# Longer stores for long rows, eight pairs shared by ScalarE and GpSimd, and short rows made on VectorE, in a store-bound kernel

## Chip, cores, metric

One core of one Trainium2 chip. The metric is the device time of one execution in microseconds (us), the median of several runs.

## The reference

For every pair (row r, column c < r) of 39 fields it forms the outer product of two 16-vectors, normalizes over the batch, and multiplies by a 16x16 weight.

```python
cross  = xj[:, rows, :, None] * xi[:, cols, None, :]         # (1024, 741, 16, 16)
mean   = jnp.mean(cross, axis=(0, 2, 3), keepdims=True)
var    = jnp.mean(jnp.square(cross - mean), axis=(0, 2, 3), keepdims=True)
normed = (cross - mean) * jax.lax.rsqrt(var + BN_EPS)
normed = normed * gamma[None, :, None, None] + beta[None, :, None, None]
out    = normed[:, :, None, :, :] * W[None, None, :, :, :]   # 777 MB in float32
```

With s and t for scale and shift of a pair, the work is `(xj * (xi * s) + t) * W`. The loads move 6 MB and the stores 777 MB, so the kernel is above all a stream of stores.

## The kernel before

The statistics take the first 40 us. Then the kernel goes through tiles (row r, two samples of each of 128 partitions). A long row r and the short row 38 - r share a *slot*: 38 pairs, one half of a double buffer in SBUF. Every pair of one sample is 1 KB per partition.

- `scale_xi` (GpSimd): xs = xi * s.
- `products`: xs * xj, 16 small operations per sample, 11 or 12 on ScalarE, the others on GpSimd.
- `finish`: (y + t) * W, one VectorE operation per pair (0.66 us); a few pairs on GpSimd instead, as one add each and one joint weighting.
- `store`: pieces of the tile as they become ready, all on SyncE's queue.

```python
def products(n):
    xs = xs_of.pop(n)
    split = E - (POOL_I_LONG if tiles[n][0] > TWO else POOL_I)
    for t in range(T):
        for i in range(E):
            product(n, nc.scalar if i < split else nc.gpsimd, t, i, xs[:, t])

def store(n, c0, c1):
    # [cut]
    step = 1 if r > ONE and c1 == r else T      # the last piece leaves sample by sample
    for t in range(0, T, step):
        nc.sync.dma_start(out_v[...], view(n)[:, t : t + step, c0:c1, :])

def bounds(n):
    # [cut: the first eight tiles]
    pieces = 1 + (r > ONE) + (r > TWO)          # ONE, TWO = 24, 31

# the main loop
    if n + 2 < len(tiles):
        scale_xi(n + 2)
    finish(n)
    # [cut]
    if n + 1 < len(tiles):
        products(n + 1)
```

In the timelines below each engine executes its own instructions in the order in which this loop emits them: GpSimd idles 8.16 us before an add while its next products stand behind it, and they start earlier when they are emitted earlier (e5).

## Time and profile before

| | before |
|---|---|
| time, median of 6 runs | 1891.22 us |
| VectorE, ScalarE, GpSimd busy | 92%, 86%, 83% |
| store queue, share of its 16 engines | 98.3% |
| DMA packets | 70288 |

An engine's busy share is an average; the row to look at first is the DMA's. A queue that is busy for 98% of the span sets the time, and an engine's idle time beside it costs nothing, until the engine delivers a store so late that the queue runs dry. The prediction below shows the lines for this.

### The profile page before, as it was taken

Reading aid. Unit: us, or ns where it says so; the run is one execution under the profiler, and the core shown is the slowest. Engines: PE = TensorE matmul, PEld = TensorE weight load, DVE = VectorE, ACT = ScalarE, POOL = GpSimd, SP = SyncE. Lnnn points to the kernel's source line nnn. Section 1 sums busy time; section 2 is a strip of 40 time slices with the busy share of each in tenths; the row PEclk is TensorE's granted clock in tenths of the full one; section 3 lists DMA queues with packets and bytes.
Section 4 is the critical chain, followed back from the end, with each engine's and each line's share of the span. In section 5 each row is a group of like instructions: output and inputs, shape, how many; then the busy total and the mean of one; then the engine's idle time right before and its main releaser. Section 6 shows DMA issues by size and latency. Waiting matters only on the chain. (4 is left out here: it accounts for less than half of the span.)

```text
span 1889.3 us, 10288 instructions
## 1 busy us (share of the span) xinstructions
PE 24.5 (1%) x128; PEld 23.1 (1%) x128; DVE 1730.7 (92%) x2612; ACT 1621.3 (86%) x3625; POOL 1574.5 (83%) x1985
## 2 busy tenths in 40 slices
PE   3100000000000000000000000000000000000000
PEld 3100000000000000000000000000000000000000
DVE  7999999998989898989898989899999999999996
ACT  8999989898989898989898989888888888888762
POOL 9798878788888888888888888888888888888972
DMA  4999999999999999999999999999999999999999
GB/s 164 390 418 429 425 427 429 430 424 429 424 425 426 424 424 426 422 425 425 424 425 423 426 423 426 422 422 422 421 421 422 418 415 419 416 419 419 415 419 390
DMA packets 70288, 783.67 MB, mean 415 GB/s; under 512 B 5057, under 2 KB 6209, under 8 KB 15937
## 3 DMA queue, kind: packets, MB, share of 16 engines
q1 hardware_dynamic: 69632, 780.46, 98.3%
q10 hardware_dynamic: 576, 2.56, 0.3%
q14 instruction: 79, 0.64, 0.1%
q8 instruction: 1, 0.02, 0.0%
HBM read 6.00 MB, written 776.99 MB: 414 GB/s over the span
## 5 line engine op out<-in xcount | busy, mean ns | idle before, releaser
L238 DVE SCALAR_TENSOR_TENSOR y_sb<-y_sb,st_sb,w_dve 128x512 f32<-128x512 f32 x2542 | 1678.5, 740 | 131.5 <-issue 128.3
L139 ACT ACTIVATE y_sb<-xs,xj_sb 128x256 f32<-128x256 f32 (+32 forms) x3544 | 1576.4, 539 | 223.5 <-DMA out_dram<-y_sb 171.8
L141 POOL TENSOR_SCALAR y_sb<-xs,xj_sb 128x560 f32<-128x560 f32 (+35 forms) x1256 | 643.2, 536 | 35.1 <-DMA out_dram<-y_sb 32.6
L230 POOL TENSOR_TENSOR y_sb<-y_sb,w_sb 128x1024 f32<-128x1024 f32 (+4 forms) x138 | 442.0, 3203 | 11.5
L159 POOL TENSOR_TENSOR xs<-xi_sb,st_sb 128x576 f32<-128x576 f32 (+37 forms) x150 | 187.8, 1252 | 225.3 <-ACT y_sb L139 217.8
L226 POOL TENSOR_SCALAR y_sb<-y_sb,st_sb 128x512 f32<-128x512 f32 x384 | 259.4, 692 | 12.9 <-ACT y_sb L139 12.9
L204 DVE TENSOR_TENSOR y_sb<-y_sb,w_dve 128x2560 f32<-128x2560 f32 (+5 forms) x8 | 21.0, 2682 | 2.3 <-ACT y_sb L194 2.3
L139 ACT ACTIVATE y_sb<-xi_sb,xj_sb 128x304 f32<-128x304 f32 x40 | 18.7, 534 | 0.1
L414 PE MATMUL ps<-y_sb 39*128 39x38 f32 (+37 forms) x76 | 16.5, 397 | 5.6 <-DVE y_sb L402 5.6
L414 PEld LDWEIGHTS ps<-y_sb 39*128 39x128 f32 x76 | 16.3, 329 | 5.8 <-issue 5.8
L194 ACT ACTIVATE y_sb<-y_sb,st_sb 128x512 f32<-128x512 f32 x20 | 14.2, 797 | 0.0
L196 POOL TENSOR_SCALAR y_sb<-y_sb,st_sb 128x512 f32<-128x512 f32 x18 | 13.5, 771 | 0.3 <-issue 0.3
L141 POOL TENSOR_SCALAR y_sb<-xi_sb,xj_sb 128x304 f32<-128x304 f32 x24 | 11.9, 518 | 0.0
L299 DVE TENSOR_REDUCE y_sb<-y_sb 128x78 f32<-128x1248 f32 x8 | 11.1, 1442 | 0.0
L277 DVE TENSOR_REDUCE y_sb<-xj_sb 128x78 f32<-128x1248 f32 (+1 forms) x5 | 5.9, 1189 | 5.6 <-DMA xj_sb<-in_r_xj_dram 5.6
L293 ACT ACTIVATE y_sb<-y_sb 128x1248 f32<-128x1248 f32 x8 | 9.9, 1243 | 1.3 <-POOL y_sb L283 1.1
L283 POOL TENSOR_TENSOR y_sb<-xj_sb,y_sb 128x1248 f32<-128x1248 f32 x4 | 9.3, 2314 | 1.9 <-ACT y_sb L327 1.9
L283 POOL TENSOR_TENSOR y_sb<-xi_sb,y_sb 128x1248 f32<-128x1248 f32 x4 | 9.3, 2318 | 0.0
L316 PE MATMUL ps<-y_sb 128*39 128x79 f32 x48 | 7.2, 339 | 16.5 <-DVE y_sb L299 16.5
L316 PEld LDWEIGHTS ps<-y_sb 128*39 128x39 f32 x48 | 6.1, 183 | 17.4 <-DVE y_sb L299 9.6
L277 DVE TENSOR_REDUCE y_sb<-xi_sb 128x78 f32<-128x1248 f32 (+1 forms) x5 | 5.9, 1186 | 0.0
L259 POOL TENSOR_SCALAR_AFFINE_SELECT y_sb<-y_sb 39x4992 f32<-39x4992 f32 x1 | 4.6, 4623 | 0.0
(45 smaller groups left out, 16.9 us busy)
## 6 DMA issues: line engine op xcount, KB each, us to landing
out_dram<-y_sb SPq DMA_DIRECT2D x32, 3072.0 KB, 13.7
out_dram<-y_sb SPq DMA_DIRECT2D x28, 2816.0 KB, 15.7
out_dram<-y_sb SPq DMA_DIRECT2D x32, 1664.0 KB, 14.2
out_dram<-y_sb SPq DMA_DIRECT2D x16, 3328.0 KB, 17.2
out_dram<-y_sb SPq DMA_DIRECT2D x30, 1536.0 KB, 15.2
out_dram<-y_sb SPq DMA_DIRECT2D x12, 3840.0 KB, 17.6
out_dram<-y_sb SPq DMA_DIRECT2D x12, 3584.0 KB, 18.1
out_dram<-y_sb SPq DMA_DIRECT2D x22, 1792.0 KB, 17.4
```

The costliest lines, as they stand in the source:

```text
L139: nc.scalar.activation(y, src, AF.Copy, scale=scale)
L141: engine.tensor_scalar(y, src, scale, 1.0, ALU.mult, ALU.mult)
L159: nc.gpsimd.tensor_tensor(xs, xi_sb[:, t0 : t0 + T, 0:r, :], s_sb[:, :, n0 : n0 + r, :].to_broadcast([P, T, r, E]), ALU.mult,)
L194: nc.scalar.activation(y[:, :, c, :], y[:, :, c, :], AF.Identity, bias=t_c, scale=s_c)
L196: nc.gpsimd.tensor_scalar(y[:, :, c, :], y[:, :, c, :], s_c, t_c, ALU.mult, ALU.add)
L204: nc.vector.tensor_tensor(y[:, :, c0:c1, :], y[:, :, c0:c1, :], w_dve.unsqueeze(1).to_broadcast([P, T, c1 - c0, EE]), ALU.mult,)
L226: nc.gpsimd.tensor_scalar(y[:, :, c, :], y[:, :, c, :], t_sb[:, n0 + c : n0 + c + 1], 1.0, ALU.add, ALU.mult)
L230: nc.gpsimd.tensor_tensor(y[:, :, split:r, :], y[:, :, split:r, :], w_sb.unsqueeze(1).to_broadcast([P, T, r - split, EE]), ALU.mult,)
L238: stt(y[:, :, c, :], y[:, :, c, :], t_sb[:, n0 + c : n0 + c + 1], w_dve.to_broadcast([P, T, EE]), ALU.add, ALU.mult,)
L283: nc.gpsimd.tensor_tensor(devs[n % 7], sources[x][:, t0 : t0 + T], shift[:, x : x + 1, :].unsqueeze(3).to_broadcast([P, T, F, E]), ALU.sub ...
L316: nc.tensor.matmul(acc[0:F, 0 : 2 * F + 1], lhs, fb[:, t], start=t == 0, stop=t == NT - 1)
L414: nc.tensor.matmul(ps[:, :, first[r] - n0 : first[r] - n0 + r], pick[:, r, :], stq[:, :, 0:r], start=True, stop=True,)
```

## The change

Its intent is fewer and longer packets at the end of the run, where rows are long, with the work redistributed so that halves are ready in time. A packet here is what one partition stores of one sample in one piece: 12 pairs are 12 KB. (1) Rows over 31 leave in halves instead of thirds. (2) In rows over 33, ScalarE adds t to eight pairs of the first half, in two fours, and GpSimd weighs them. (3) VectorE scales and multiplies rows 1 to 4 itself, from copies of s and xj in PSUM, with an own buffer. In rows 32 and 33 ScalarE also takes 12 of 16 products again, instead of 11. Cut to its core:

```diff
-ONE, TWO = 24, 31
+ONE, LONG = 24, 33
-POOL_SHARE = 0.13
+POOL_SHARE, POOL_PAIRS_LONG = 0.13, 8
+SHORT = 4
 ...
     def products(n):
+        if r <= SHORT:
+            xs = scaled_short.tile(...)
+            nc.vector.tensor_tensor(xs, xi_sb[...], s_short[...], ALU.mult)
+            for t in range(T):
+                nc.vector.tensor_tensor(view(n)[:, t]..., xs[:, t]..., xj_short[...], ALU.mult)
+            return
 ...
-        split = E - (POOL_I_LONG if tiles[n][0] > TWO else POOL_I)
+        split = E - (POOL_I_LONG if tiles[n][0] > LONG else POOL_I)
 ...
-        pieces = 1 + (r > ONE) + (r > TWO)
+        pieces = 1 + (r > ONE)
 ...
     def finish(n):
-        split = r - int(r * POOL_SHARE + 0.5)
-        for c in range(split, r):
-            nc.gpsimd.tensor_scalar(...)                  # add t
-        if split < r:
-            nc.gpsimd.tensor_tensor(y[:, :, split:r, :], ...)   # weigh
+        long = r > LONG
+        p1 = r // 2 if long else r
+        p0 = p1 - (POOL_PAIRS_LONG if long else int(r * POOL_SHARE + 0.5))
+        step = POOL_PAIRS_LONG // 2 if long else r
+        for c0 in range(p0, p1, step):
+            c1 = min(c0 + step, p1)
+            for c in range(c0, c1):
+                if long:
+                    nc.scalar.activation(y[:, :, c, :], ..., AF.Identity, bias=t_c)
+                else:
+                    nc.gpsimd.tensor_scalar(...)          # add t
+            nc.gpsimd.tensor_tensor(y[:, :, c0:c1, :], ...)     # weigh
         ...
         def apply(group):
-            nc.vector.tensor_mul(st_sb[:, 0, n0:n1], ps[:, 0], st_sb[:, 0, n0:n1])
+            nc.vector.tensor_mul(ps[:, 0], ps[:, 0], st_sb[:, 0, n0:n1])
+            nc.vector.tensor_copy(st_sb[:, 0, n0:n1], ps[:, 0])
 ...
         affine(0)
+        nc.scalar.copy(xj_short, xj_sb[:, :, 1 : SHORT + 1, :])
```

More of the change, by code (lines that the diff above doesn't have):

```diff
@@ L75, in tile_pair_outer_batchnorm @@
     cpool = ctx.enter_context(tc.tile_pool(name="cpool", bufs=1))
+    scaled_short = ctx.enter_context(tc.tile_pool(name="scaled_short", bufs=1))
     scaled = ctx.enter_context(tc.tile_pool(name="scaled", bufs=2))
@@ L124, in tile_pair_outer_batchnorm @@
     ps_s, ps_c, ps_g = banks[0], banks[1], banks[2:5]
+    s_short = ps_g[0]
+    xj_short = ps_c.rearrange("p (t r i) -> p t r i", t=NT, i=E)
     ps_st = banks[5:7] + ps_g
@@ L167, in products @@
     def products(n):
+        r, t0, _ = tiles[n]
+        if r <= SHORT:
+            xs = scaled_short.tile([P, T, r, E], F32, tag="xs_short", name=f"xs_{r}_{t0}")
+            nc.vector.tensor_tensor(
+                xs,
+                xi_sb[:, t0 : t0 + T, 0:r, :],
+                s_short[:, first[r] : first[r] + r]
+                .unsqueeze(1)
+                .unsqueeze(3)
+                .to_broadcast([P, T, r, E]),
+                ALU.mult,
+            )
+            for t in range(T):
+                nc.vector.tensor_tensor(
+                    view(n)[:, t].rearrange("p n (i j) -> p n i j", j=E),
+                    xs[:, t].unsqueeze(2).to_broadcast([P, r, E, E]),
+                    xj_short[:, t0 + t, r - 1 : r, :].unsqueeze(3).to_broadcast([P, r, E, E]),
+                    ALU.mult,
+                )
+            return
         xs = xs_of.pop(n)
-        split = E - (POOL_I_LONG if tiles[n][0] > TWO else POOL_I)
+        split = E - (POOL_I_LONG if tiles[n][0] > LONG else POOL_I)
         for t in range(T):
@@ L223, in finish @@
         y = view(n)
-        split = r - int(r * POOL_SHARE + 0.5)
-        for c in range(split, r):
-            nc.gpsimd.tensor_scalar(
-                y[:, :, c, :], y[:, :, c, :], t_sb[:, n0 + c : n0 + c + 1], 1.0, ALU.add, ALU.mult
-            )
-        if split < r:
+        long = r > LONG
[5 more added lines that the diff above has]
+            for c in range(c0, c1):
+                t_c = t_sb[:, n0 + c : n0 + c + 1]
+                if long:
+                    nc.scalar.activation(y[:, :, c, :], y[:, :, c, :], AF.Identity, bias=t_c)
+                else:
+                    nc.gpsimd.tensor_scalar(
+                        y[:, :, c, :], y[:, :, c, :], t_c, 1.0, ALU.add, ALU.mult
+                    )
             nc.gpsimd.tensor_tensor(
-                y[:, :, split:r, :],
-                y[:, :, split:r, :],
-                w_sb.unsqueeze(1).to_broadcast([P, T, r - split, EE]),
+                y[:, :, c0:c1, :],
+                y[:, :, c0:c1, :],
+                w_sb.unsqueeze(1).to_broadcast([P, T, c1 - c0, EE]),
                 ALU.mult,
@@ L236, in finish @@
         for c0, c1 in zip(bounds(n), bounds(n)[1:]):
-            for c in range(c0, min(c1, split)):
+            for c in [*range(c0, min(c1, p0)), *range(max(c0, p1), c1)]:
                 stt(
```

## The prediction

> **What bounds the kernel now.** I read the page's first parts, then the busy time by stretches, the waits, the timeline of one slot and the groups by form. First the busy shares and the DMA rows of the page:
>
> ```profile
> PE 24.5 (1%) x128; PEld 23.1 (1%) x128; DVE 1730.7 (92%) x2612; ACT 1621.3 (86%) x3625; POOL 1574.5 (83%) x1985
> ...
> DMA  4999999999999999999999999999999999999999
> GB/s 164 390 418 429 425 427 429 430 424 429 424 425 426 424 424 426 422 425 425 424 425 423 426 423 426 422 422 422 421 421 422 418 415 419 416 419 419 415 419 390
> ...
> q1 hardware_dynamic: 69632, 780.46, 98.3%
> ```
>
> Three engines are over 80% busy, but the queue that stores the output is at 98.3% of its 16 engines for the whole span. The bound is DMA: 777 MB have to leave. Only the start and whatever each packet costs can be saved. The stretches (columns: DVE, ACT, POOL busy near the middle, then PE clock, DMA share, GB/s) say where the rate changes:
>
> ```profile
> 300.00:500.00 200.00, 0.00 (x0) 0.00 (x0) 188.15 (x288) 182.63 (x412) 167.14 (x215) 1.00 1.00 427
> ...
> 1420.00:1512.00 92.00, 0.00 (x0) 0.00 (x0) 83.95 (x128) 75.87 (x180) 80.48 (x104) 1.00 1.01 420
> ...
> 1700.00:1795.00 95.00, 0.00 (x0) 0.00 (x0) 86.58 (x132) 74.69 (x161) 84.55 (x98) 1.00 1.00 417
> ```
>
> The DMA share stays 1.00 to the end while GB/s falls from 427 to 417: the queue is not starved in the late rows, its packets are smaller. So the engines' waits are mostly waits for the queue's buffers:
>
> ```profile
> ACT y_sb L139 <- DMA out_dram<-y_sb: 171.8, 58, 8.7
> DVE y_sb L238 <- issue: 128.3, 52, 6.0
> ```
>
> One slot (36 pairs of row 36 and 2 of row 2, one half of the double buffer) in the timeline:
>
> ```profile
> 1646.78 19.85 ACT L139 ACTIVATE y_sb<-xs,xj_sb 128x576 f32<-128x576 f32 x46 [3.52 <-DMA out_dram<-y_sb]
> 1661.63 21.81 DVE L238 SCALAR_TENSOR_TENSOR y_sb<-y_sb,st_sb,w_dve 128x512 f32<-128x512 f32 x33 [1.55 <-issue]
> 1661.68 2.21 POOL L159 TENSOR_TENSOR xs<-xi_sb,st_sb 128x1184 f32<-128x1184 f32 x1 [2.52 <-ACT y_sb L139]
> 1663.87 3.35 POOL L226 TENSOR_SCALAR y_sb<-y_sb,st_sb 128x512 f32<-128x512 f32 x5
> 1667.31 5.61 POOL L230 TENSOR_TENSOR y_sb<-y_sb,w_sb 128x2560 f32<-128x2560 f32 x1
> 1672.88 2.13 POOL L141 TENSOR_SCALAR y_sb<-xs,xj_sb 128x32 f32<-128x32 f32 x8
> 1675.31 7.35 POOL L141 TENSOR_SCALAR y_sb<-xs,xj_sb 128x592 f32<-128x592 f32 x10
> ```
>
> ScalarE waits until the half's last-but-one store has landed, makes the products, and at 1661.6 (call this E: all products of the long row exist) VectorE finishes pairs for 21.81 us. The next E is at 1685.6: one slot is 24 us, which is what its 10 MB need.
>
> **What the Trainium skill says.** "DMA: Bandwidth & Descriptors", section "Where 436 GB/s comes from", puts the fabric's ceiling at 435.2 GB/s; the trace agrees, 427 here. Its section "Why small descriptors are slow (HBM only)" gives a fixed overhead of about 3 cycles per packet; the trace's packet records show a larger one: 12 KB take 467.1 ns, 18 KB 693.0, 24 KB 920.8, so 37.8 ns per KB and some 12.7 ns besides. "ScalarE: Activation LUTs", section "What ACT_TABLE_LOAD costs", gives 186 ns + 0.833 per element, 93 more for each pointer operand, 93 less back to back: 706 ns for 512 elements with two pointers. The 20 such ones of the trace (L194) were busy 14.2 us, 710 each, so it agrees; the new add has one pointer, about 614 ns. "SBUF — State Buffer", section "SBUF: two separate sides", says that GpSimd and a VectorE operation with two SBUF inputs exclude each other. That is why the short rows get s and xj in PSUM. The trace has no slowdown from the present pairing (the weighting of 2560 elements takes 5.60 or 5.61 us beside a busy VectorE), and I expect none from the new one.
>
> **The change part by part.** (1) *Halves.* Rows 25 to 31 already leave in two pieces; rows 32 to 38 go from three to two. Row 38: 12+13+13 KB cost 467.1 + 2x504.7 = 1476.5 ns per partition and sample; 19+19 KB cost 2x731 (between 693.0 for 18 KB and 769.0 for 20 KB) = 1462. The seven rows save 14.5, 14.9, 15.3, 15.2, 15.1, 14.4 and 14.0 ns, together 103.4. There are 1024 samples, spread over 16 engines: 103.4 x 64 = **-6.6 us**, straight off the bound.
>
> (2) *Longer way to the first store, rows 34 and up.* Now ScalarE adds t to 8 pairs in two fours, GpSimd weighs each four, and the first half waits for both. From the groups by form:
>
> ```profile
> L139 ACT ACTIVATE y_sb<-xs,xj_sb 128x544 f32<-128x544 f32 x66 | 42.5, 734 | 11.7 <-DMA out_dram<-y_sb 7.9 <-POOL y_sb L230 3.8
> L141 POOL TENSOR_SCALAR y_sb<-xs,xj_sb 128x544 f32<-128x544 f32 x30 | 20.9, 714 | 0.0
> L230 POOL TENSOR_TENSOR y_sb<-y_sb,w_sb 128x2048 f32<-128x2048 f32 x4 | 18.1, 4512 | 0.3
> L230 POOL TENSOR_TENSOR y_sb<-y_sb,w_sb 128x512 f32<-128x512 f32 x4 | 5.1, 1272 | 0.3
> ```
>
> Four adds 2.5 us (estimate above), two weightings of 2048 elements 2 x 4.51: the first store goes out at E+11.7, where the present one (11 or 12 pairs at 0.66 us, 21.81/33) goes at E+7.3 to 8.2. Is that hidden? The margin is the time from the landing of the store that frees the half to the moment the queue reaches the slot's first piece, less the slot's own chain. The issue and landing records give it for the present kernel: the first store is issued 8.0 us (row 34), 5.4 (row 36) and 4.7 (row 38) before the preceding one lands, of which about 2 are issue and receipt. After, row 38: one sample's last half, 19 pairs, 5.9 us, plus one tile 23.4, less receipt 0.9 = 28.4; the chain is 0.1 + 15.3 products + 11.7 + 1.2 = 28.3. So margin 0.1 for row 38; likewise 1.2 for 37, 1.8 for 36, 3.4 for 34. Thin, but not negative. I charge **+1 us**.
>
> (3) *Short rows on VectorE.* It removes 24 small ScalarE and 8 small GpSimd products per short tile and lets ScalarE's eight adds (4.9 us) fit. VectorE has 26 + 3 finishes for row 34 with its short row 4, two products of 1024 elements (1.22 us, as the weighting of that size, L204) and a scaling of some 0.3: 19.2 + 2.7 = 21.9 us, as before. But the order of instructions has a trap **at row 34 alone**: row 4 is the one short row with a pair for GpSimd (0.13 x 4 rounds to 1). GpSimd's stream is now: scaled row, two weightings, add for the short pair *waiting for VectorE's short products*, its weighting, then the ten products of the next long row. VectorE gets to the short products only after its 26 long finishes. So: E + 17.2 (26 x 0.66) + 2.8 (scaling, two products) + 2.1 (add 0.69, weighting 1.27, wait) + 7.0 (10 x 0.697, from 20.9/30) = E + 29.1 to the next E, where the queue needs 23.6 for the slot. Four such steps (34 to 34 three times, 34 to 35 once) lose 5.5 each = 22; the margin at the first of them is about 4 (3.4 by the working above, and row 5 before it is larger). Idle DMA: **+18 us**. From row 35 on the short rows have no GpSimd pair, and GpSimd's next products end at E+11.7+7.3 = E+19, before they are needed.
>
> (4) *Start.* The extra VectorE copies of s fall into its waits; the copy of xj to PSUM (512 elements) delays ScalarE, which is never idle from 40 to 142 us, by some 0.6, while the queue is not yet full (0.87 and 0.91 of it used from 40 to 80). **+0.5 us.** Rows 32 and 33 give ScalarE 24 products instead of 22 (1.3 us) and margins of some 3 us remain.
>
> Sum: 1891.2 - 6.6 + 1 + 18 + 0.5 = 1904.1, rounded to 1904.
>
> **Rivals.** *Everything is hidden*: if the short pair's wait at row 34 is absorbed, what is left is the packet saving, 1885 to 1886. For it: the queue's share is 1.00 throughout, and engines off the bound cost nothing. Against it: 29 is more than 23.6, four times running, and only two halves exist. *The later first store starves the queue in all of rows 35 to 38*: with margins of 0.1 to 2 us, 2 us of extra latency (a slower add, a GpSimd weighting that collides with VectorE) would cost about half to one us per slot on 16 slots, besides the 18: 1912 to 1920. For it: the thin margin; against it: durations in the trace are very steady. *VectorE is relieved and this shortens the end*: it would need VectorE to be the bound; its 0.66 us finishes are waited for only because the buffers are. No more than 1 us.
>
> **Range and chances.** The GpSimd stall is read from program order and measured durations; I give it 85%. Its size is uncertain by some 3 us (margin, four waits), the rest by 2. All hidden has 10%, starved throughout 5%. 80% range 1896 to 1910. Every case lies between -0.4% and +1.6%, so within 2% is nearly certain: 0.97, faster by over 2% 0.01, slower 0.02.
>
> **What would show it.** Right: some 7600 fewer packets (28 stores fewer, each 256 packets and some markers); GpSimd's add for the short pair waits about 8 us for VectorE's products four times; VectorE's first finish waits 6 to 7 us for GpSimd's products four times around 1430 to 1530; DMA share dips there by some 18 us in all, and stays at 1.00 in rows 35 to 38. Wrong: no dip (then the time is near 1886 and row 34's margin was larger), or a dip in rows 36 to 38 (the first store is later than E+11.7), or long weightings beside the short products (the two exclude each other after all).

## The result, and the profile after

| | before | after |
|---|---|---|
| time, median of 6 runs | 1891.22 us | 1904.35 us (1904.15 to 1904.70) |
| store queue, share | 98.3% | 97.2% |
| DMA packets | 70288 | 62666 |

The ratio is 1.007 (95% interval 1.0057 to 1.0082), so the change costs 13 us.

The page of the changed kernel, its DMA rows:

```profile
DMA  4999999999999999999999999999997899999999
GB/s 166 387 418 427 426 427 427 428 426 430 427 424 424 424 424 425 424 424 425 425 424 425 424 427 424 417 425 423 420 420 332 351 401 421 424 424 427 425 417 413
...
q1 hardware_dynamic: 62016, 780.46, 97.2%
```

Two things are to be seen. The last slices now run at up to 427 GB/s, where they ran at 415 to 419: the packets are longer. And slices 31 to 33 have a hole (332, 351, 401), which was not there. The stretch of the hole holds four slots, from the first store of the first row-34 tile to that of the first row-35 tile. The same four slots before and after (columns: DVE, ACT and POOL busy, PE clock, DMA share, GB/s):

```profile
1406.00:1501.00 95.00, 0.00 (x0) 0.00 (x0) 86.95 (x132) 79.58 (x184) 83.09 (x110) 1.00 1.01 421
```

```profile
1408.00:1524.00 116.00, 0.00 (x0) 0.00 (x0) 87.44 (x130) 79.73 (x125) 80.23 (x61) 1.00 0.83 350
```

95 us became 116, with no engine any busier: the work is the same, the waiting isn't. The waits of the changed kernel name it (columns: us in total, times, longest):

```profile
POOL y_sb L267 <- ACT y_sb L262: 75.2, 20, 8.4
...
ACT y_sb L262 <- POOL y_sb L147: 35.1, 4, 9.9
POOL y_sb L264 <- DVE y_sb L190: 32.6, 4, 8.2
DVE y_sb L275 <- POOL y_sb L147: 28.3, 4, 7.2
```

L264 is GpSimd's add for a pair, L190 VectorE's products of a short row, L147 GpSimd's share of the products, L275 VectorE's finishing, L262 ScalarE's new adds, L267 GpSimd's weighting. Three of the waits occur four times each, in a ring. One turn of it in the timeline of the changed kernel:

```profile
1442.85 0.28 DVE L180 TENSOR_TENSOR xs<-xi_sb,ps 128x128 f32<-128x128 f32 x1
1443.16 2.35 DVE L190 TENSOR_TENSOR y_sb<-xs,ps 128x1024 f32<-128x1024 f32 x2
1445.55 2.06 DVE L275 SCALAR_TENSOR_TENSOR y_sb<-y_sb,st_sb,w_dve 128x512 f32<-128x512 f32 x3
1445.62 0.69 POOL L264 TENSOR_SCALAR y_sb<-y_sb,st_sb 128x512 f32<-128x512 f32 x1 [8.16 <-DVE y_sb L190]
1446.39 1.27 POOL L267 TENSOR_TENSOR y_sb<-y_sb,w_sb 128x512 f32<-128x512 f32 x1
1447.64 6.97 POOL L147 TENSOR_SCALAR y_sb<-xs,xj_sb 128x544 f32<-128x544 f32 x10
1454.58 2.04 POOL L167 TENSOR_TENSOR xs<-xi_sb,st_sb 128x1088 f32<-128x1088 f32 x1
1454.65 5.01 ACT L262 ACTIVATE y_sb<-y_sb,st_sb 128x512 f32<-128x512 f32 x8 [9.85 <-POOL y_sb L147]
1454.65 17.21 DVE L275 SCALAR_TENSOR_TENSOR y_sb<-y_sb,st_sb,w_dve 128x512 f32<-128x512 f32 x26 [7.04 <-POOL y_sb L147]
```

VectorE makes the products of row 4 (1443.16 to 1445.51). Only then can GpSimd add t to the last pair of row 4, after 8.16 us of idling; then it weighs that pair, and only then, at 1447.64, starts its ten product operations for the next row-34 tile, 6.97 us. All of that tile waits for them until 1454.6: VectorE 7.04 us, ScalarE 9.85. The next such turn starts its finishing at 1483.58, 28.93 us later. By their packets' records (17, 17 and 4 KB take 656.0, 656.0 and some 164 ns, 256 of each over 16 engines) the queue needs 23.6 us for such a slot.

In the kernel before, the pair of row 4 stood at the same place in GpSimd's stream, but its input came from ScalarE and from GpSimd itself and was ready. GpSimd went through without idling (L226 is the add, L230 the weighting, L141 the products of the next tile):

```profile
1482.10 0.69 POOL L226 TENSOR_SCALAR y_sb<-y_sb,st_sb 128x512 f32<-128x512 f32 x1
1482.88 1.28 POOL L230 TENSOR_TENSOR y_sb<-y_sb,w_sb 128x512 f32<-128x512 f32 x1
1484.12 7.10 POOL L141 TENSOR_SCALAR y_sb<-xs,xj_sb 128x560 f32<-128x560 f32 x10
```

### The profile page after: what moved, and what is told of

Its sections match the earlier page's. It is cut to its first block, busy times and chain, and to the rows that moved or that the text cites. A ratio compares the mean times of both kernels' runs of the same rounds, so it can differ in the third digit from the quotient of the medians. Undisturbed runs are those within 1.5% of the kernel's fastest.

```text
span 1902.7 us, 9617 instructions
## 1 busy us (share of the span) xinstructions
PE 24.5 (1%) x128; PEld 23.1 (1%) x128; DVE 1718.9 (90%) x2602; ACT 1647.8 (87%) x3418; POOL 1535.8 (81%) x1749
## 2 busy tenths in 40 slices
DMA packets 62666, 783.63 MB, mean 412 GB/s; under 512 B 4608, under 2 KB 5760, under 8 KB 15488
## 3 DMA queue, kind: packets, MB, share of 16 engines
q1 hardware_dynamic: 62016, 780.46, 97.2%
## 5 line engine op out<-in xcount | busy, mean ns | idle before, releaser
L275 DVE SCALAR_TENSOR_TENSOR y_sb<-y_sb,st_sb,w_dve 128x512 f32<-128x512 f32 x2478 | 1637.8, 741 | 153.1 <-issue 111.8
L145 ACT ACTIVATE y_sb<-xs,xj_sb 128x320 f32<-128x320 f32 (+20 forms) x3176 | 1502.5, 566 | 177.9 <-DMA out_dram<-y_sb 154.4
L147 POOL TENSOR_SCALAR y_sb<-xs,xj_sb 128x352 f32<-128x352 f32 (+25 forms) x1112 | 600.2, 566 | 38.6 <-DMA out_dram<-y_sb 35.9
L267 POOL TENSOR_TENSOR y_sb<-y_sb,w_sb 128x2048 f32<-128x2048 f32 (+3 forms) x158 | 514.9, 3264 | 85.1 <-ACT y_sb L262 75.2
L167 POOL TENSOR_TENSOR xs<-xi_sb,st_sb 128x576 f32<-128x576 f32 (+33 forms) x134 | 183.0, 1366 | 181.9 <-ACT y_sb L145 175.8
L264 POOL TENSOR_SCALAR y_sb<-y_sb,st_sb 128x512 f32<-128x512 f32 x288 | 195.7, 695 | 32.7 <-DVE y_sb L190 32.6
L262 ACT ACTIVATE y_sb<-y_sb,st_sb 128x512 f32<-128x512 f32 x160 | 100.2, 708 | 36.6 <-POOL y_sb L147 35.1
L190 DVE TENSOR_TENSOR y_sb<-xs,ps 128x1024 f32<-128x1024 f32 (+3 forms) x32 | 24.8, 817 | 0.6
L222 ACT ACTIVATE y_sb<-y_sb,st_sb 128x512 f32<-128x512 f32 x20 | 14.3, 805 | 0.0
L224 POOL TENSOR_SCALAR y_sb<-y_sb,st_sb 128x512 f32<-128x512 f32 x18 | 13.6, 774 | 0.5 <-issue 0.5
L147 POOL TENSOR_SCALAR y_sb<-xi_sb,xj_sb 128x304 f32<-128x304 f32 x24 | 11.9, 531 | 0.0
L353 PE MATMUL ps<-y_sb 128*39 128x79 f32 x48 | 7.2, 339 | 16.6 <-DVE y_sb L336 16.6
L353 PEld LDWEIGHTS ps<-y_sb 128*39 128x39 f32 x48 | 6.1, 183 | 17.5 <-DVE y_sb L336 9.5
```

The source lines that it names most:

```text
L145: nc.scalar.activation(y, src, AF.Copy, scale=scale)
L147: engine.tensor_scalar(y, src, scale, 1.0, ALU.mult, ALU.mult)
L167: nc.gpsimd.tensor_tensor(xs, xi_sb[:, t0 : t0 + T, 0:r, :], s_sb[:, :, n0 : n0 + r, :].to_broadcast([P, T, r, E]), ALU.mult,)
L190: nc.vector.tensor_tensor(view(n)[:, t].rearrange("p n (i j) -> p n i j", j=E), xs[:, t].unsqueeze(2).to_broadcast([P, r, E, E]), xj_short ...
L222: nc.scalar.activation(y[:, :, c, :], y[:, :, c, :], AF.Identity, bias=t_c, scale=s_c)
L262: nc.scalar.activation(y[:, :, c, :], y[:, :, c, :], AF.Identity, bias=t_c)
```

## The experiments

All kernels gave the reference's result. The kernel before ran beside them at 1891.16 to 1891.21 us.

| run | what it is | median us | ratio to before |
|---|---|---|---|
| after | the change | 1904.35 | 1.0070 |
| e1_dve_pair | GpSimd's pair of row 4 given to VectorE | 1885.37 | 0.9969 |
| e5_pair_later | same work, GpSimd's pair of row 4 after the next products | 1885.41 | 0.9969 |
| e3_halves_only | before, with halves alone | 1886.39 | 0.9975 |
| e2_short3 | row 4 back to ScalarE and GpSimd | 1888.48 | 0.9985 |
| e6_thirds | e1 with thirds again | 1890.87 | 0.9998 |
| e4_pair_every_short | after, with a GpSimd pair in rows 1 to 3 too | 1974.26 | 1.0439 |
| e7_whole31 | e1, rows 25 to 31 whole per sample | 1898.49 | 1.0038 |
| e8_whole_all | e1, all rows over 24 whole per sample | 1981.48 | 1.0477 |
| e9_whole27 | e1, rows 25 to 27 whole per sample | 1884.96 | 0.9967 |

### e1_dve_pair: take the pair away from GpSimd

```diff
-        p0 = p1 - (POOL_PAIRS_LONG if long else int(r * POOL_SHARE + 0.5))
+        p0 = p1 - (POOL_PAIRS_LONG if long else int(r * POOL_SHARE + 0.5) * (r > SHORT))
```

> The changed kernel, but VectorE finishes all four pairs of row 4; GpSimd gets none of the short rows. Theory (GpSimd's pair of row 4 waits for VectorE and holds up the next long row's products): the four waits and the dip of DMA share around 1420 to 1530 us are gone, the time falls by the 17.5 us of idle queue to 1886 to 1888. Rival (the later first store starves the queue, or the VectorE products of row 4 are themselves too slow): the dip stays, 1898 or more, since neither is touched and VectorE even gets four pairs more.

1885.37 us (1885.02 to 1885.71), 19.0 us less than the change as it was. The hole is gone from the page of this run; slices 31 to 33 are at 423 to 426:

```profile
GB/s 162 386 420 424 428 427 427 431 424 425 431 423 424 426 424 426 423 425 424 424 425 425 425 424 423 421 425 423 418 422 423 424 426 423 424 418 418 424 416 413
```

Four pairs moved from GpSimd (an add and a weighting each) to VectorE (one operation each), and the whole loss went with them. The rivals (late first store, slow products of row 4) would have left it: both are still in this kernel.

### e5_pair_later: the same work in another order

e1 leaves open whether GpSimd had too much to do at row 34 or did it in the wrong order. Here nothing changes engine; only the finish of row 4's tiles is emitted behind the next long row's products.

```diff
-            finish(n)
+            late = tiles[n][0] == SHORT
+            if not late:
+                finish(n)
 ...
                 products(n + 1)
+            if late:
+                finish(n)
```

> The changed kernel with the same work on the same engines; only the order is another: the finish of row 4's tile is emitted after the next long row's products, so GpSimd's pair no longer stands ahead of them. Theory (order, not load): no wait for GpSimd's products at row 34, 1886 to 1888. Rival (GpSimd or VectorE has too much to do at row 34): still 1900 or more.

1885.41 us, the same as e1. In its timeline GpSimd's ten products now come first, and the add (L264) idles 1.31 us instead of 8.16:

```profile
1431.83 6.95 POOL L147 TENSOR_SCALAR y_sb<-xs,xj_sb 128x544 f32<-128x544 f32 x10
1437.33 0.28 DVE L180 TENSOR_TENSOR xs<-xi_sb,ps 128x128 f32<-128x128 f32 x1
1437.64 2.35 DVE L190 TENSOR_TENSOR y_sb<-xs,ps 128x1024 f32<-128x1024 f32 x2
1440.03 2.06 DVE L275 SCALAR_TENSOR_TENSOR y_sb<-y_sb,st_sb,w_dve 128x512 f32<-128x512 f32 x3
1440.09 0.69 POOL L264 TENSOR_SCALAR y_sb<-y_sb,st_sb 128x512 f32<-128x512 f32 x1 [1.31 <-DVE y_sb L190]
```

So it is the order, not the load: an engine that executes in order stood before an operation whose input came late, with urgent work behind it.

### e4_pair_every_short: more of the suspected cost

```diff
-        p0 = p1 - (POOL_PAIRS_LONG if long else int(r * POOL_SHARE + 0.5))
+        p0 = p1 - (POOL_PAIRS_LONG if long else max(1, int(r * POOL_SHARE + 0.5)))
```

> The changed kernel with the suspected cost given to rows 3, 2 and 1 as well: GpSimd gets one pair of each short row. Theory: from one E to the next 29.1 us (row 35), 29.3 (36), 29.6 (37) instead of 23.5, so 12 more steps lose 5.6 to 6.1 us each, 69 us: 1970 to 1977. Rival (row 34's loss has another cause): at most a few us more than 1904, since GpSimd gets 12 adds and 12 weightings of 2 us in all each, beside a queue that is the bound.

1974.26 us, 69.9 more than the change, where 69 was worked out. Its waits show the ring turning sixteen times instead of four:

```profile
ACT y_sb L262 <- POOL y_sb L147: 150.7, 16, 9.8
DVE y_sb L275 <- POOL y_sb L147: 132.1, 16, 9.6
POOL y_sb L264 <- DVE y_sb L190: 130.6, 16, 8.4
```

Twelve pairs whose own work on GpSimd is 2 us each cost 5.8 us each.

### e2_short3: undo the third part for row 4 alone

```diff
-SHORT = 4
+SHORT = 3
-    xj_short = ps_c.rearrange("p (t r i) -> p t r i", t=NT, i=E)
+    xj_short = ps_c[:, : NT * SHORT * E].rearrange("p (t r i) -> p t r i", t=NT, i=E)
```

> The changed kernel with only rows to 3 on VectorE; row 4's products go back to ScalarE and GpSimd, and GpSimd keeps its pair of row 4. Theory: the pair then waits for ScalarE's small products, which are done well before VectorE's long finishes, so no stall of 5.5 us: 1885 to 1888 (ScalarE has 14.2 + 5.0 + 5.4 us a slot at row 34, a us over the queue's 23.6, which a margin of some 2 us covers). Rival (GpSimd's pair of row 4 is harmful wherever its products are made): 1900 or more.

1888.48 us, just above the expected range. GpSimd keeps its pair of row 4, and the ring is gone. What is left is ScalarE's load: first stores of row 34 came 24.9 us apart (1433.41, 1458.30, 1483.20), a slot of the queue being 23.6, and the queue stood still for 1.6 us before row 35. Between the first two of these stores ScalarE is busy for 24.80 of 24.89 us (`prof e2_short3 --windows 1433.41:1458.30`). So once ScalarE makes the adds, it pays to take the small products of row 4 from it: 3.1 us between e2 and e1. VectorE is one place for them; no other was tried.

### e3_halves_only and e6_thirds: what the packets are worth

e3 is the kernel before with `pieces = 1 + (r > ONE)` and nothing else; e6 is e1 with `pieces = 1 + (r > ONE) + (r > 31)`.

> The kernel before with nothing but its first part: rows over 31 leave in halves instead of thirds. Theory (the saving is the packets'): 6.6 us less than before, 1884 to 1886, some of it lost at row 38, whose first store goes out after 19 VectorE pairs (12.6 us) with a margin of about -1 us. Rival (halves only pay with the earlier end that parts two and three bring, as the first store is late): 1890 or more, with idle in the DMA share of rows 36 to 38.

> The first experiment's kernel (VectorE finishes all of row 4) with rows over 31 back in thirds: 7168 packets more, all else equal. Theory (12.7 ns a packet over 16 engines): 6.6 us more than that kernel's 1885.4, 1892, with the same DMA share. Rival (the gain is the fewer stores' waits or an earlier end): within 2 us of 1885.4.

Halves alone give 4.8 us (1886.39). Thirds put back into e1 cost 5.5 us (1890.87 against 1885.37). The packet arithmetic had said 6.6. (The expectation of e6 mixes two figures: 7168 packets of 12.7 ns over 16 engines are 5.7 us; 6.6 us are 14.8 ns a packet, which is what the prediction's 103.4 ns over seven rows come to.) The direction and most of the size are the packets', and the rest can be read in the packet records of e6 and e1: e6's packets took 6.8 us more in all (over 16 engines, with small marker packets), but overlapped by 1.5 us more, so that a packet's recorded time is not all its own; and its engines idled 0.6 us more. That is 5.9 us, where the two profiled executions differ by 5.8. In e3 row 38 has less margin, as expected: its first stores are issued only 1.7 to 0.7 us before the preceding ones land, and before the last two of its four tiles the 16 engines idle 0.6 and 0.75 us on average. Two stretches of e3 near the end (the DMA share is the last figure but one; the second stretch holds the end of the run, where the engines idle 1.3 us because no further store follows):

```profile
1795.00:1842.00 47.00, 0.00 (x0) 0.00 (x0) 43.23 (x67) 29.70 (x44) 35.12 (x33) 1.00 0.98 419
1842.00:1884.00 42.00, 0.00 (x0) 0.00 (x0) 23.68 (x36) 4.00 (x6) 8.95 (x6) 1.00 0.96 408
```

The second and third part of the change (ScalarE's adds, short rows on VectorE) are worth the 1.0 us between e3 and e1, no more.

### e7_whole31, e8_whole_all, e9_whole27: still longer packets

If packets are what counts, a row could leave in one piece per sample. `pieces = 1 + (r > 31)`, `1` and `1 + (r > 27)` in e1.

> The first experiment's kernel with rows 25 to 31 in one piece for each sample (two stores, packets of 25 to 31 KB) instead of halves. Theory: 7 rows x 12.7 ns x 64 = 5.7 us less packet time, and a margin that stays over zero (row 31: 36.4 us of queue against a chain of 35.9, counting that ScalarE now waits 2 us for the second sample's store): 1879 to 1881. Rival (the first store, at E+18 instead of E+10, starves the queue): 1885 or more, with idle queue before the first store of rows 29 to 31.

> As the last, but every row over 24 in one piece for each sample, up to row 38. It takes 12.3 us of packet time away and makes the margin negative on purpose. Working as in the prediction (queue time from the freeing store to the slot, less the chain): row 33 -2.5, 34 -0.6, 35 -2.0, 36 -3.5, 37 -4.8, 38 -6.4 us for two slots, so half of that for each of 24 slots, 39 us of idle queue: 1885 - 12 + 39 = 1912, at least 1900. If the margin is not what decides (the queue takes what comes), 1873 to 1875.

Both expectations failed on size: 1898.49 instead of 1880, and 1981.48 instead of 1912. In e7 the time lies where the rival had put it, but the idle sits at the changes of row and not at every slot. The margin inside a row was about right. In e8, the queue stands still 4.0 and 3.8 us before the second and fourth slot of row 37, where -4.8 for two slots was worked out, and 3.9, 1.3 and 3.7 us before the second to fourth of row 38, where -6.4 for two was. What the working had left out is the *change of row*. A tile lies sample by sample, so when r grows by one, the first sample's region takes in the first pair of the old second sample. With halves that pair left with the first piece. With whole samples it leaves last, and ScalarE waits for it. The timeline of e7 at its first row-31 slot:

```profile
1108.69 21.17 ACT L145 ACTIVATE y_sb<-xs,xj_sb 128x496 f32<-128x496 f32 x48 [9.36 <-DMA out_dram<-y_sb]
```

The store that it waits for is the second sample of row 30, which landed at 1108.59. Before the first slot of rows 28 to 31 the 16 engines of the queue idled 1.4, 3.3, 4.7 and 6.5 us on average in e7 (the expectation of e9 below counts a little otherwise); in e8 6.5 to 8.9 us before that of rows 32 to 38. This settles the size too: up to the first slot of row 34, e7's engines idle 18.9 us more than e1's, and 16.6 of them are at the changes to rows 27 to 31.

> The first experiment's kernel with only rows 25 to 27 in one piece for each sample. In the run with rows 25 to 31 so, the queue stood still before the first slot of each new row (1.8, 2.4, 4.1 and 6.5 us for rows 28 to 31, under 0.7 for 25 to 27), because a longer row's first sample reaches into pairs of the second sample's store. Theory: three rows save 3 x 0.81 = 2.4 us of packets and lose about 1 us: 1883 to 1885. Rival (whole rows lose steadily, at every row): 1886 or more.

1884.96 us (1884.70 to 1885.17), within the expected range. It was run on another chip. It is the lowest median, but e1's runs reach down to 1885.02, so that 0.4 us is not a gain that is shown. e1, e5 and e9 are the fastest versions; they beat the kernel before by 0.3%.

## Why the prediction was right, step by step

**The number.** 1904 was predicted and 1904.35 measured; the mechanism behind the largest term is right. That the sum came within 0.4 us is luck. The packet records of the two profiled executions account for their difference (idle time is the mean of the 16 DMA engines, in us):

| term | predicted | measured |
|---|---|---|
| packets: recorded time -6.8, less overlap +1.4 | -6.6 | -5.4 |
| idle in the first 100 us | +0.5 | +0.5 |
| idle from there to row 34 | 0 | +1.8 |
| idle in row 34 | +18 | +21.4 |
| idle in rows 35 to 38 | +1 | -3.8 |
| idle after the last store's issue | 0 | -1.2 |
| sum | +12.9 | +13.3 |

The first, third and fourth terms came out 1.2, 1.8 and 3.4 us above their predictions, the last two 4.8 and 1.2 us below.

**Halves, -6.6.** The number of packets fell by 7622 where 7600 was predicted. The new 19 KB packet took 730.6 ns, predicted by interpolation as 731. The worth on the clock was 5.5 us (e6) rather than 6.6. The 1.8 us up to row 34 belong here: e3, which has the halves alone, idles as long there, e6, with thirds, doesn't.

**Longer way to the first store, +1.** The margin nearly held: in rows 35 to 38 of the changed kernel the queue as a whole never stood still. In row 38 the first store was issued 1.5 to 3.4 us before the preceding landing (0.1 us was the worked-out margin), and one of them was late: before the third tile, issued 1.94 us ahead, 13 of the 16 engines had run dry, 1.0 us of idle time on average. In all these rows the engines idled 1.2 us, but in the same rows of the kernel before 5.0 us, so that net the charge was not due. Durations were as taken: eight adds 5.01 us, 626 ns each, where the figures of "ScalarE: Activation LUTs", section "What ACT_TABLE_LOAD costs", give about 613 (the prediction has 614). "SBUF — State Buffer", section "SBUF: two separate sides", was not contradicted: the weighting of 2048 elements on GpSimd took 4.51 us before and 4.53 after, beside a VectorE that reads one operand from PSUM.

**Row 34, +18.** Measured: 28.93 us from one start of finishing to the next (29.1 predicted); four waits of 8.15 us on average for VectorE (about 8), four of 7.1 us for GpSimd's products (6 to 7). From the end of the last packet to the start of the next, the queue stood still 1.8, 5.3, 4.5 and 5.5 us before the four first stores (the expectation of e1 has 17.5 us for their sum). That understates the loss, because the 16 DMA engines don't run dry together: before the first of these stores 12 of them had nothing to do from 1433.0 us on, while one worked until 1436.6 and the landing came at 1437.0. As a mean over the engines the four steps lost 4.9, 5.4, 5.3 and 5.5 us. So the 5.5 us of each step was right, and the mis-sized part of +18 is the margin of 4 us at the first step. It was read from landings, which come when the slowest engine is done, and it saved about half a us. e5 measures the whole as 18.9 us, since its engines idle 2.4 us more in rows 35 to 38 than those of the changed kernel. The small stops there and in e1 (0.2 to 1.3 us) also fall where a first store is issued while only the slower engines still have packets. Why the engines drift apart stays open.

**Start, +0.5.** Idle time of the 16 engines in the first 100 us rose from 30.6 to 31.1 us.

**The rivals.** *Everything is hidden* (1885 to 1886) is what e1 and e5 show as soon as the pair's order is mended: it failed on one operation in a stream. *The queue starves in all late rows* didn't occur. *VectorE is relieved* is bounded by the 1.0 us between e3 and e1. One slip in the prediction's text: of the timeline lines that it shows for a slot of row 36, the last but one is GpSimd's part of row 2 and the last its part of the next slot's row 37. Another: of the two lines shown as waits for the queue's buffers, the second names `issue`, not the queue, and the page's longest total (GpSimd's scaling on ScalarE, 217.8 us) isn't shown. A third: the 4.7 us for row 38 is the largest of its four tiles (4.7, 4.5, 4.3 and 3.5). The argument doesn't rest on them.

## What to carry to other kernels

In a kernel that one queue bounds, an engine off the bound costs nothing until an operation at the head of its stream waits for another engine's late result: then look at what stands *behind* it. So when work moves between engines, check for each engine in program order what each operation waits for and what urgent work follows; four pairs with 2 us of GpSimd's work each cost 19 us here, and moving them behind the next products took all of it back. A margin worked out from landing to first store tells roughly how much later a store may be issued. It flatters, since a landing is that of the slowest DMA engine, and it has to be worked out where the layout changes too, not only in the steady state.

## What the Trainium skill lacked or had wrong

- "DMA: Bandwidth & Descriptors", section "Why small descriptors are slow (HBM only)", speaks of about 3 cycles per packet and of packets to 256 B. Here a packet is 10 to 24 KB, the packet records put some 12.7 to 14.8 ns on each, and 7168 packets more cost 5.5 us (e6 against e1), that is 12.3 ns each on one of 16 engines.
- No page that I looked up tells how late a store may be issued before a busy queue runs dry. In the changed kernel a first store issued 2.5 us before the preceding one landed followed without idle engines (row 37), one issued 1.9 us before left 1.0 us of mean idle time (row 38), one issued 0.5 us after it 4.9 us, with the whole queue still for 1.8 (row 34). No fixed lead time follows: in e1 one issued 2.5 us before left 1.0 us (row 37).
